# Router logits as four 32-column products in the attention's product bank, then one turn, in a relative-attention and mixture-of-experts kernel

## The chip, the cores and the metric

The kernel runs on one core of one Trainium2 chip. The time of a run is the device time in microseconds from the first to the last instruction and the little that lies around them. Three runs of the kernel before gave 1938.45, 1939.77 and 1939.66 us, median 1939.66 us. PE is the matrix engine (PEld its weight loads), DVE the vector engine, ACT the scalar engine, POOL the general engine, SP the engine that only issues transfers.

## The reference, cut to what matters

The input is 16 sequences (B) of 512 rows of 128 numbers, all float32. Each row goes through attention with relative positions, and then through a layer in which one of 16 experts is chosen for each row:

```python
x = x + _layernorm(attention(_layernorm(x)))          # 16 heads of 8, relative keys and values
h = _layernorm(x)                                     # rows of 128
logits = h @ w_router.T                               # [rows, 16]
_, top_idx = jax.lax.top_k(logits, 1)
scores = jax.nn.sigmoid(logits) * one_hot(top_idx)    # only the chosen expert's score is left
gate_up = (scores * h) @ gate_up_proj[expert]
expert_out = (up * silu(gate)) @ down_proj[expert]
shared = silu(h @ w_gate.T) * (h @ w_up.T) @ w_down.T
x = x + _layernorm(shared + expert_out)
```

The change is about the line of `logits`: 512 rows by 128 numbers by 16 experts for each sequence.

## The kernel before, in words

**Two stages.** The attention stage fills most of the span. It also chooses the experts ("the route") and scatters each row to a table in memory that is ordered by expert. The second stage reads that table in 73 blocks of 128 rows and runs the experts. The change lies in the first stage alone.

**The steps.** A sequence `b` is cut into 4 pieces `c` of 128 queries and each piece into 4 parts `n`, so it has 16 steps, `k` = 0 to 15, and the loop at L760 runs 256 steps and 24 more that empty the pipeline. The order of the instructions on every engine is that of the program (class `InOrder`, L39): no scheduler moves anything. In step `i` PE does, in this order:

- the scores of step `i` (`scores`, L375): four products `ps<-km,qb` of 32 rows by 512, and then 16 short products `ps<-relk,qr` for the relative keys;
- the first eight turns (transposes) of the weights of step `i - 1` (`turn`, L418), `pt<-ident,w`;
- the output products of step `i - 5` (`attend`, L471): 16 values' products `pa<-wT,v`, which show as 32 records of a 32-column tile (a float32 product takes two passes, a turn takes one), and 24 small products `pa<-wT,relv` for the relative values (`attend_near`, L503), 48 records;
- eight more turns;
- one extra that depends on `k` (L773 to L789, `spare`): the next sequence's projections, the turn of the reciprocal sums (`prt`), or the output projection (`py`, `output`, L538);
- what the route asks for (L833 to L847).

DVE meanwhile finds four maxima (`nmax`), copies two of the turned tiles out (`wT`), and takes in what `attend` made: `od`, `oz` and the sum `oT` (L494 to L499). ACT takes the exponentials and copies the other two turned tiles.

**The bank.** The scores have five PSUM buffers and the turned tiles two, but everything else shares a single one, the pool `ps_o` with `bufs=1` (L102, `bank`, L218). `attend` writes three thirds of it: `every3[:, 0]` for the values' products, `every3[:, 2]` for the relative values, and `every3[:, 1]` for `join_places`. Whoever takes the bank next waits until DVE has read it.

**The model for the new products.** In each step with `n == 1`, `attend` is given a finished piece `done`, and `join_places` (L459) runs four products of 128 rows by 32 columns, one to each 32-partition strip of `every3[:, 1]`, between the values' products and the relative values' products. DVE copies the result to `oj` between `oz` and `oT`. In the same step, after the second eight turns, `output` reads `oj` on PE.

**The route.** `route` (L595) is a generator for one sequence, which the loop advances at set steps. For sequences 0 to 13 (`r[0] < B - 2`, L837) the fifth call, at the end of step `k = 10` of the next sequence, is `turn_x2` (L639): four turns of the normalized rows, which ACT copies to `x2T`. The sixth, at the end of step `k = 11`, is `logits` (L648): four products with `x2T` as the loaded operand (128 columns each) and the 16 columns of `wr` streamed past it, into `pl`, which DVE copies to `lg`. Later calls find the largest logit, count the rows of each expert (`places`) and scatter the rows by indirect transfers that POOL issues (`rows<-pay,at_i`), of which two run in the steps 9 and 11 of the sequence after. The last two sequences follow another timetable. What follows `lg` is the same for all.

Of the kernel before, what the change touches and what calls it, by code (L numbers as in the profile page):

```python
# [9 lines left out]
F32 = mybir.dt.float32  # L10
# [7 lines left out]
P = 128  # L18
# [10 lines left out]
NC = P // 32  # L29
NE = 16  # L30
# [20 lines left out]
def relative_attention_then_moe(  # L51
# [6 lines left out]
    nc = tc.nc  # L58
    B = x.shape[0]
# [6 lines left out]
    ident = const.tile([P, P], F32, name="ident")  # L66
# [27 lines left out]
    with ExitStack() as actx:  # L94
        wp = actx.enter_context(tc.tile_pool(name="attn_w", bufs=1))
        dp = actx.enter_context(tc.tile_pool(name="attn_dram", bufs=1, space=DRAM))
        bp = actx.enter_context(tc.tile_pool(name="attn_batch", bufs=2))
# [5 lines left out]
        pe, act, dve, sp_q, pool = (InOrder(tc, e) for e in (nc.tensor, nc.scalar, nc.vector, nc.sync, nc.gpsimd))  # L103
# [68 lines left out]
        def later_loads():  # L172
            sp_q.dma_start(vext[0:127, :], rel_v[0:1, :].to_broadcast([127, HD]))
            sp_q.dma_start(vext[127 : 127 + NR, :], rel_v)
            sp_q.dma_start(vext[384:LR, :], rel_v[NR - 1 : NR, :].to_broadcast([LR - 384, HD]))
            va = vext[:, :]
            sp_q.dma_start(
                relv.rearrange("p t d -> p (t d)"),
                bass.AP(va.tensor, va.offset, [[HD, P], [1, 384 * HD]]),
            )  # L180
            sp_q.dma_start(wo, WoT)
            wo_v = WoT.rearrange("(g h d) o -> h g d o", g=HG, h=HH)
            for h in range(HH):
                for g in range(HG):
                    r = h * 32 + g * HD
                    sp_q.dma_start(wo_h[r : r + HD, :], wo_v[h, g])
            sp_q.dma_start(bo_r, bo.partition_broadcast(P))
            sp_q.dma_start(wr, w_routerT)


        mh = wp.tile([P, H], F32, name="mh")
# [22 lines left out]
        msum = wp.tile([P, HG, HD], F32, name="msum")  # L214

        batch, wts = {}, {}

        def bank(shape, name):  # L218
            return ps_o.tile(shape, F32, tag="o", name=name)
# [239 lines left out]
        def join_places(pj, b, c):  # L459

            oz = batch.pop((b, c, "oz"))
            for h in range(HH):
                pe.matmul(
                    pj[h * 32 : (h + 1) * 32, :], msum.rearrange("p g d -> p (g d)"),
                    oz[:, h].rearrange("p n t q -> p (n t q)"), start=True, stop=True,
                )
            oj = up.tile([P, P], F32, tag="oj", name=f"oj{b}_{c}")
            batch[b, c, "oj"] = oj
            return lambda: dve.tensor_copy(oj, pj)

        def attend(b, c, n, done=None):  # L471


            wT = wts[b, c][0]
            v = batch[b]["v"]
            Rh = batch[b, c, "R"][0]
            if n == 0:
                batch[b, c, "oT"] = up.tile([P, NKT * 4, TQ], F32, tag="oT", name=f"oT{b}_{c}")
            oT = batch[b, c, "oT"]
            every3 = bank([P, 3, P], f"pa{b}_{c}_{n}")  # L480
            pa = every3[:, 0]
            for kt in range(NKT):
                vn = 1 if kt <= n - 2 else 2 if kt >= n + 2 else 0
                for g in range(HG):
                    r = slice(g * 32, (g + 1) * 32)
                    pe.matmul(
                        pa[r, :], v[:, vn, kt, r], wT[:, n, g, (kt - n) % NKT, :],
                        start=(kt == 0), stop=(kt == NKT - 1),
                    )
            t = slice(n * 4, n * 4 + 4)  # L490
            summed = join_places(every3[:, 1], *done) if done is not None else lambda: None
            near_done = attend_near(every3[:, 2], b, c, n)

            def leave():  # L494
                od = up.tile([P, 4, HH, TQ], F32, tag="od", name=f"od{b}_{c}_{n}")
                dve.tensor_mul(od, pa.rearrange("p (t h q) -> p t h q", h=HH, q=TQ), Rh[:, t])
                near_done()
                summed()
                dve.tensor_reduce(oT[:, t], od.rearrange("p t h q -> p t q h"), AX.X, ALU.add)  # L499

            return leave
# [54 lines left out]

        wr = wp.tile([P, NE], F32, name="wr")
        order = wp.tile([P, NE], F32, name="order")  # L560
        nc.gpsimd.iota(order, [[-1, NE]], base=NE, channel_multiplier=0, allow_small_or_imprecise_dtypes=True)
        ids = wp.tile([P, NT], I32, name="ids")
# [32 lines left out]
        def route(b, c0=0, c1=NC):  # L595
# [5 lines left out]
            nc_, pieces, nm = c1 - c0, slice(c0, c1), f"{b}_{c0}"  # L601
# [34 lines left out]
            yield  # L636
            x2T = bp.tile([P, nc_ * P], F32, tag="x2T", name=f"x2T{nm}", bufs=1)

            def turn_x2():  # L639
                pt = bank([P, nc_ * P], f"ptf{nm}")  # L640
                for t in range(nc_):
                    pe.transpose(pt[:, t * P : (t + 1) * P], x2[:, t, :], ident)
                return lambda: act.copy(x2T, pt)

            yield turn_x2
            lg = sp.tile([P, nc_, NE], F32, tag="lg", name=f"lg{nm}")

            def logits():  # L648
                pl = bank([P, nc_, NE], f"pl{nm}")
                for t in range(nc_):  # L650
                    pe.matmul(pl[:, t, :], x2T[:, t * P : (t + 1) * P], wr, start=True, stop=True)
                return lambda: dve.tensor_copy(lg, pl)

            yield logits

            shape = [P, nc_, NE]
            mx = sp.tile([P, nc_], F32, tag="mx", name=f"mx{nm}")
# [98 lines left out]
        if B > 1:  # L756
            load_x(1)
        later_loads()
        routes = {}
        for i in range(total + 24):  # L760
            b, c, n = at(i)
# [4 lines left out]
            done = at(i - 9)[:2] if n == 1 and 0 <= i - 9 < total else None  # L766
# [3 lines left out]
            if 0 < b < B and k == 6:  # L770
                routes[b - 1, 0] = route(b - 1)

            if i == total + 1:  # L773
                routes[b - 1, 0] = route(b - 1, 0, NC - 1)
            if i == total + 5:
                routes[b - 1, 1] = route(b - 1, NC - 1, NC)
# [7 lines left out]
            if nxt is not None:  # L784
                if k == 0 and b + 2 < B:
                    load_x(b + 2)
                if k in (6, 7, 14, 15):
                    f = {6: x_turn, 7: queries, 14: keys, 15: values}[k]
# [17 lines left out]
            if old is not None:  # L806
                attend(*at(old), done=done)()
            elif done is not None:
                join_places(bank([P, P], f"pj{b}"), *done)()
# [44 lines left out]
    with ExitStack() as fctx:  # L854
        wp = fctx.enter_context(tc.tile_pool(name="ffn_w", bufs=1))
# [7 lines left out]
        pe, act, dve, pool = (InOrder(tc, e) for e in (nc.tensor, nc.scalar, nc.vector, nc.gpsimd))  # L863
# [182 lines left out]
```

## Time and profile before

| What | Value |
|---|---|
| Median of three runs | 1939.66 us |
| The profiled execution | 1937.03 us, span 1935.3 us |
| Granted PE clock, mean of the span | 0.989 |
| Busy PE, DVE, ACT, POOL | 1867.6, 1528.0, 1208.7, 992.1 us |
| PE busy from 100 to 1600 us | 1492.89 us |
| `pl<-wr,x2T` on PE | 128 records, 16.6 us |
| `pa<-oz,msum` on PE | 504 records, 25.3 us |
| `lg<-pl` on DVE | 17 copies, 3.8 us |

Busy time is the time in which at least one instruction of the engine runs, so products that overlap are counted once. A group's mean duration is longer than the distance from one record to the next, as the products are pipelined; the distance is what a record costs, and is read from the starts in the timeline. "Idle before" is the time in which the engine stood still ahead of a group, with the instruction that ended the wait. "Issue" stands for a wait that the profile ties to nothing.

The steps are very regular. Taken from the starts of `ps<-km,qb`, the step `k = 12` lasts 6.15 us in each of the 16 sequences, and the sixteen steps of a sequence add up to about 102.6 us.

### The profile page before, as it was taken

The page shows a single profiled execution, that of the slowest core. Times are in us where ns is not written, and L with a number is a line of the kernel's source. Part 1 is how long each engine was busy: PE and PEld are TensorE (multiplying, and loading weights), DVE is VectorE, ACT ScalarE, POOL GpSimd, SP SyncE. Part 2 cuts the span into 40 slices and gives each one's busy share as a digit, 9 for nine tenths or more (in the row PEclk, how much of TensorE's full clock was granted, in tenths as well). Part 3 has the DMA queues.
Part 4 walks back from the last instruction along what each step waited for, and adds up shares of the span by engine and source line. Part 5 has one row for each costly group of instructions (what it writes and reads, how often), then busy time and mean ns, then how long its engine had stood idle before and what let it go on. Part 6 is the DMA issues. An engine that isn't in the chain of part 4 may idle for free. (4 is left out here: it accounts for less than half of the span.)

```text
span 1935.3 us, 88211 instructions
## 1 busy us (share of the span) xinstructions
PE 1867.6 (96%) x38254; PEld 1391.1 (72%) x38254; DVE 1528.0 (79%) x3995; ACT 1208.7 (62%) x3077; POOL 992.1 (51%) x1388
## 2 busy tenths in 40 slices
PE   6999999999999999999999999999999999779997
PEld 3667767777776777676767677777767676579997
DVE  4777787878787878787888878787879787757776
ACT  3666666666666666666666666666666665257775
POOL 4345455545454554546454555454645544236666
PEclk9999999999999999999999999999999999879999
DMA  2312000000000000000000000000000000066663
GB/s 77 69 31 52 4 24 4 17 12 11 17 5 24 5 24 3 25 3 25 3 24 5 24 4 20 9 13 16 5 18 4 18 3 9 8 172 182 183 180 89
DMA packets 88327, 68.64 MB, mean 35 GB/s; under 512 B 26439, under 2 KB 74340, under 8 KB 87808
## 3 DMA queue, kind: packets, MB, share of 16 engines
q1 hardware_dynamic: 81248, 53.60, 10.4%
q0 software_dynamic: 4384, 8.57, 1.3%
q8 instruction: 301, 4.93, 1.1%
q10 hardware_dynamic: 2304, 0.80, 0.2%
q14 instruction: 90, 0.74, 0.1%
HBM read 44.79 MB, written 18.75 MB: 33 GB/s over the span
## 5 line engine op out<-in xcount | busy, mean ns | idle before, releaser
L47 ACT ACTIVATE w<-ps,nmax 128x512 f32<-128x512 f32 x1024 | 700.1, 694 | 561.9 <-DVE nmax L47 561.4
L47 DVE TENSOR_REDUCE nmax<-ps 128x1 f32<-128x512 f32 x1024 | 655.7, 682 | 229.2 <-PE ps L47 228.0
L47 PE MATMUL pt<-ident,w 128*128 128x128 f32 x4096 | 561.5, 280 | 4.6 <-DVE wT L47 4.0
L47 PEld LDWEIGHTS pt<-ident,w 128*128 128x128 f32 x4096 | 439.1, 141 | 125.5 <-issue 85.6
L47 DVE COPY wT<-pt 128x512 f32<-128x512 f32 x512 | 348.7, 681 | 0.7 <-PE pt L47 0.7
L47 ACT COPY wT<-pt 128x512 f32<-128x512 f32 x512 | 301.6, 589 | 25.1 <-PE pt L47 23.4
L47 PE MATMUL ps<-km,qb 32*128 32x512 f32 x2048 | 297.7, 645 | 3.5 <-POOL qb L47 3.5
L47 PEld LDWEIGHTS ps<-relk,qr 64*32 64x32 f32 x8192 | 124.3, 106 | 226.6 <-issue 184.1
L47 PE MATMUL pa<-wT,v 128*32 128x128 f32 x8192 | 276.7, 276 | 2.5 <-DVE oz L47 1.4
L47 PE MATMUL ps<-relk,qr 64*32 64x288 f32 (+4 forms) x8192 | 274.8, 377 | 0.0
L47 PEld LDWEIGHTS pa<-wT,v 128*32 128x32 f32 x8192 | 208.1, 109 | 45.3 <-issue 37.1
L47 ACT ACTIVATION_READ_ACCUMULATOR w<-ps,nmax 128x1 f32 x1024 | 211.9, 207 | 0.0
L47 PE MATMUL pa<-wT,relv 128*32 128x48 f32 (+1 forms) x12288 | 199.4, 211 | 6.6 <-issue 6.5
L47 POOL TENSOR_TENSOR Rh<-R,mh 128x512 f32<-128x512 f32 x64 | 66.7, 1042 | 263.8 <-ACT R L47 263.8
L47 PEld LDWEIGHTS pa<-wT,relv 128*32 128x32 f32 x12288 | 187.7, 110 | 10.8 <-issue 10.8
L47 POOL TENSOR_TENSOR qr<-qz,mq 128x1024 f32<-128x1024 f32 x64 | 137.4, 2147 | 0.0
L47 PEld LDWEIGHTS ps<-km,qb 32*128 32x128 f32 x2048 | 82.5, 184 | 58.6 <-issue 32.0
L47 POOL TENSOR_SCALAR km<-kT,kend 128x32 f32<-128x32 f32 (+2 forms) x223 | 116.4, 524 | 1.7 <-PE ps L47 0.9
L47 POOL COPY km<-kT 128x32 f32<-128x32 f32 (+3 forms) x207 | 53.6, 263 | 113.8 <-ACT kT L47 113.8
L47 POOL DMA_INDIRECT out_dram<-f,to x73 | 75.9, 1040 | 46.1 <-issue 32.3
L47 POOL COPY rb<-rt 128x512 f32<-128x512 f32 x64 | 39.4, 616 | 114.9 <-DVE rt L47 114.7
L47 DVE TENSOR_TENSOR od<-pa,Rh 128x128 f32<-128x128 f32 x256 | 73.2, 286 | 30.4 <-PE pa L47 26.9
(162 smaller groups left out, 2341.7 us busy)
## 6 DMA issues: line engine op xcount, KB each, us to landing
gu<-_L_ffn_gate_up_proj_dram SPq DMA_DIRECT2D x73, 256.0 KB
dn<-in_L_ffn_down_proj_dram SPq DMA_DIRECT2D x73, 128.0 KB
rows<-zero SPq DMA_DIRECT2D x19, 266.0 KB
xc<-rows SPq DMA_DIRECT2D x8, 532.0 KB
x_sb<-in_L_attn_x_dram SPq DMA_DIRECT2D x64, 64.0 KB
qd<-qp SPq DMA_DIRECT2D x16, 256.0 KB
qz<-qd SPq DMA_DIRECT2D x248, 16.0 KB
relv<-vext SPq DMA_DIRECT2D x1, 1536.0 KB
```

Of the source, the lines that this page charges most:

```text
L47: return lambda *a, **k: self.tc.keep_in_program_order(op(*a, **k))
```

## The change

For the sequences 0 to 13 the logits are made in another way:

- `wr` becomes 32 columns wide; the 16 new ones are zero (a memset on POOL at the start), and the load of the router's weights fills the first 16.
- When `turn_x2` runs, it puts `logits_tiles` on a list, `riders`. The next `attend` without a piece to join takes it: four products with `wr` (32 columns) as the loaded operand and the 128 columns of each quarter of `x2T` streamed past it, one to each strip of the free third of the bank, behind the values' products and ahead of the relative values' products of step 11. The result is the logits with experts as rows.
- DVE copies that third, 128 by 128, to a new tile `lgT`, between `oz` and `oT` of the same step.
- At the place of the old `logits`, one turn of `lgT` puts rows back as rows, and DVE copies the 16 real columns of each quarter to `lg`.

The order of the changed program has, for each of the 14 sequences, the four products and the turn on PE in place of the four old products, and one copy more on DVE. On POOL there is the one memset more, on ACT and SP nothing differs.

```diff
-            sp_q.dma_start(wr, w_routerT)
+            sp_q.dma_start(wr[:, 0:NE], w_routerT)
...
+        riders = []
...
             t = slice(n * 4, n * 4 + 4)
-            summed = join_places(every3[:, 1], *done) if done is not None else lambda: None
+            summed = lambda: None
+            if done is not None:
+                summed = join_places(every3[:, 1], *done)
+            elif riders:
+                summed = riders.pop()(every3[:, 1])
             near_done = attend_near(every3[:, 2], b, c, n)
...
-        wr = wp.tile([P, NE], F32, name="wr")
+        wr = wp.tile([P, 32], F32, name="wr")
+        nc.gpsimd.memset(wr, 0.0)
...
+            lgT = bp.tile([P, P], F32, tag="lgT", name=f"lgT{nm}", bufs=1) if b < B - 2 else None
+
+            def logits_tiles(pn):
+
+                for t in range(NC):
+                    pe.matmul(
+                        pn[t * 32 : (t + 1) * 32, :], wr, x2T[:, t * P : (t + 1) * P], start=True, stop=True
+                    )
+                return lambda: dve.tensor_copy(lgT, pn)
+
             def turn_x2():
+                if b < B - 2:
+                    riders.append(logits_tiles)
                 pt = bank([P, nc_ * P], f"ptf{nm}")
...
-                    pe.matmul(pl[:, t, :], x2T[:, t * P : (t + 1) * P], wr, start=True, stop=True)
+                    pe.matmul(pl[:, t, :], x2T[:, t * P : (t + 1) * P], wr[:, 0:NE], start=True, stop=True)
                 return lambda: dve.tensor_copy(lg, pl)
 
-            yield logits
+            def turn_logits():
+                pl = bank([P, NC, 32], f"pl{nm}")
+                pe.transpose(pl.rearrange("p c e -> p (c e)"), lgT, ident)
+                return lambda: dve.tensor_copy(lg, pl[:, :, 0:NE])
+
+            if b < B - 2:
+                yield turn_logits
+            else:
+                yield logits
```

## The prediction

> **What bounds the kernel now.** I read the windows by stage first, then PE's groups, then the timeline of the step that is changed. In the windows, from 100 to 1600 us (columns: window, length, then busy time of PE, PEld, DVE, ACT, POOL) PE is busy for 1492.89 of 1500 us, DVE for 1233.70:
>
> ```profile
> 100.00:1600.00 1500.00, 1492.89 (x33268) 1068.36 (x33270) 1233.70 (x3174) 963.72 (x2475) 780.99 (x1026) 1.00 0.06 14
> ```
>
> So in this stretch a PE microsecond more or less should be a microsecond of the span. Busy time alone doesn't prove that, so here is a second look: step 11 of sequence 6, PE in order of time (start, length, group, count).
>
> ```profile
> 704.96 1.14 PE L47 MATMUL ps<-km,qb 32*128 32x512 f32 x8
> ...
> 707.87 1.08 PE L47 MATMUL pa<-wT,v 128*32 128x128 f32 x32
> 708.77 0.38 PE L47 MATMUL pa<-wT,relv 128*32 128x64 f32 x16
> 709.33 0.62 PE L47 MATMUL pa<-wT,relv 128*32 128x48 f32 x32 [0.18 <-issue]
> 709.88 1.09 PE L47 MATMUL pt<-ident,w 128*128 128x128 f32 x8
> 710.81 0.96 PE L47 MATMUL pl<-wr,x2T 128*128 128x16 f32 x8
> 711.70 1.14 PE L47 MATMUL ps<-km,qb 32*128 32x512 f32 x8
> ```
>
> The step runs from 704.96 to 711.70, 6.74 us. In sequence 1 the same step runs from 192.21 to 198.54, 6.33 us, as it has no pause in the relv products (there 196.01 to 196.69; here 708.77 to 709.88, 0.43 longer). Yet step 12 behind it lasts 6.15 us in both (198.54 to 204.69; 711.70 to 717.85). PE time that is spared in step 11 is thus kept: nothing in step 12 waits for another engine to catch up. That is the reason why I count PE's starts and little else.
>
> **What the change removes.** Four products, eight records. From the start of pl at 710.81 to the next ps at 711.70 they hold PE for **0.89 us** (sequence 1: 197.62 to 198.54, 0.92).
>
> **What it adds on PE: the products.** The nearest row has the same shapes, loaded 128x32, streamed 128x128, four strips, at the same place between v and relv: `pa<-oz,msum`. In step 9 of sequence 6:
>
> ```profile
> 694.61 1.08 PE L47 MATMUL pa<-wT,v 128*32 128x128 f32 x32
> 695.50 0.40 PE L47 MATMUL pa<-oz,msum 128*32 128x128 f32 x8
> 695.72 0.28 PE L47 MATMUL pa<-wT,relv 128*32 128x64 f32 x5
> 696.20 0.77 PE L47 MATMUL pa<-wT,relv 128*32 128x64 f32 x43 [0.20 <-issue]
> 696.91 1.09 PE L47 MATMUL pt<-ident,w 128*128 128x128 f32 x8
> 697.92 0.46 PE L47 MATMUL py<-wo,oT 128*128 128x128 f32 x2
> ```
>
> 695.50 to 695.72: **0.22 us** for eight records, since the strips run beside each other. The ends: 0.22 by distance, 0.40 by busy time (25.3 us for 63 sets); I take the distance, as the next group starts there.
>
> **The pause.** Steps 9 and 11 hold an "issue" pause in their relv products, from sequence 2 on, and in both a `rows<-pay,at_i` of POOL starts just before: at 694.92 in step 9, at 708.17 in step 11, about 0.6 to 0.7 us ahead of the end of the v products. Sequence 1 has neither the transfer nor the pause. Relv takes 1.19 us with it in step 9 (695.72 to 696.91) against 0.68 without (step 13: 722.19 to 722.87), 0.51 more; in step 11 it is 0.43 more. After the change step 11 is laid out like step 9, products first, so I give it step 9's pause: **0.08 us** more. Ends: the pause is missed altogether (-0.43), or is as long as in the longest step 9 (7.31 us against the usual 7.13 to 7.14 by the starts of ps): +0.26.
>
> **The turn.** One more 128x128 pass behind eight like it. From 709.88 to 710.81 a pass takes 0.93 / 8 = 0.12; four prt passes ahead of ps take 0.53 (717.32 to 717.85), so the last one before ps costs 0.53 - 3 x 0.11 = **0.20 us**, and the single turn is such a last one.
>
> **The wait that it adds.** The turn reads lgT, so PE waits for DVE. What DVE does in step 11 now, and in step 9, where oj stands at lgT's place:
>
> ```profile
> 709.99 0.29 DVE L47 TENSOR_TENSOR od<-pa,Rh 128x128 f32<-128x128 f32 x1 [0.16 <-PE pa L47]
> 710.20 0.28 DVE L47 TENSOR_TENSOR oz<-pa,Rz 128x128 f32<-128x128 f32 x1
> 710.39 0.38 DVE L47 TENSOR_REDUCE oT<-od 128x32 f32<-128x128 f32 x1
> 710.69 0.68 DVE L47 COPY wT<-pt 128x512 f32<-128x512 f32 x1
> ```
>
> ```profile
> 697.49 0.28 DVE L47 COPY oj<-pa 128x128 f32<-128x128 f32 x1
> ```
>
> od moves by 0.22 + 0.08 to 710.29, oz to 710.50, lgT to 710.69 (at oT's distance), and ends 0.28 later at 710.97. In step 9 oj ends at 697.77 and py starts at 697.92, so DVE's end to PE's start takes 0.15: the turn can start at 711.12. PE has done its eight turns at 709.88 + 0.30 + 0.93 = 711.11. The wait is **0.01 to 0.02 us**. Its ends are 0 and 0.15, what it would be if the turns in between were 0.13 shorter; it is small only because eight turns cover the DVE chain. Queued behind the waiting turn is all of PE, ps of step 12 first.
>
> **What DVE pays.** lgT's copy takes 0.20 by distance. It delays oT and the wT copy, so with the 0.30 above wT ends at 711.87 and lg, rt follow by 712.2. rt feeds POOL's rb (0.61) and that prt, which PE reaches about 5.6 us into step 12: over 4 us of slack. The turned tile's buffer is wanted again by the first pt of step 12, some 2.1 us into it, and is free by 0.6. The next nmax starts 1.8 us into step 12. All hidden; if that cover were gone, 0.2 a sequence, 2.8 us in all.
>
> **Nothing else.** The memset on POOL (0.11) falls ahead of a 1.85 us idle time (before lx_rs at 7.57). The wr load has as many bytes as before. x2T is there 0.8 us into step 11, the products come 3.8 us in. Sequences 14 and 15 and the expert stage only start earlier.
>
> **The sum.** For sequences with the pause, 13 of the 14: -0.89 + 0.22 + 0.08 + 0.20 + 0.01 = -0.38. For the first, which has none: -0.92 + 0.22 + 0.20 + 0.02 = -0.48. Together 13 x 0.38 + 0.48 = **5.4 us**. The profiled execution has a span of 1935.3 and took 1937.03, so its like would take 1931.6. It ran 2.6 us below the median of the runs, and from the median, 1939.66, the forecast is **1934.3 us**.
>
> **A rule that speaks against it.** The eight products' loads span 0.24 us in step 9's PEld rows though each lasts 0.110, so loads and passes overlap. The Trainium skill, TensorE: Matmul & The Clock Gate, Part 3 (packing small matmuls), says that a weight load overlaps with running products only where the row group differs, and all four strips here use all 128 rows. By that rule this change is the last rival below; the trace disagrees with it, 0.22 us for eight.
>
> **The rivals.**
> - *The pause is as now, or is missed* (0.17). Then 13 x 0.46 + 0.48 = 6.5 us are spared, 1933.2; without any pause 13 x 0.89 + 0.48 = 12, 1927.6. For it: the pause hits one spot in time, and 0.22 us of other products now stand in front of relv. Against: step 9, laid out the same, is hit in every sequence from 2 on.
> - *The pause grows* (0.09). It falls where PE's instructions are shortest (relv, 14 ns apart), and there are 16 more ahead of them (loads counted). With the longest step 9's +0.26 in place of 0.08: 13 x 0.20 + 0.48 = 3.1 us spared, 1936.6.
> - *PE time isn't what counts, or the products don't ride in step 11* (0.04). Then the time stays at 1939.7. Against: step 12's equal length, and the order of the changed instructions, which has them there.
> - *The strips run one after another* (0.02), which ends slower. Each pass would take its load and itself, 0.110 + 0.273 = 0.38, eight 3.06 instead of 0.22, so 2.84 - 0.38 = 2.5 more a sequence, 14 x 2.5 = 34 us, 1974. It is slower from the point where the eight take over 0.60. Against: 63 sets of oz products at 0.22.
>
> **How the numbers follow.** The forecast has 0.68. About 0.2% (3.9 us) is what a measurement can tell from no change, so faster means below 1935.8. The forecast and the first rival are faster, 0.85; the second and third are the same, 0.13; the last is slower, 0.02. The range for 8 in 10 takes in the first rival's unchanged pause and part of its missed one, and the grown pause: 1931.2 to 1936.8.
>
> **What would show it.** In the changed profile: a group `pa<-x2T,wr` (or its like) of 112 records and some 5.6 us busy; `pl<-wr,x2T` left with 16 records; step 11 from ps to ps at 6.36 instead of 6.74, and 5.85 in sequence 1; step 12 still 6.15; PE idle before the new turn under 0.05 each; relv in step 11 at about 1.19. Wrong would be: a step 12 that grows by what step 11 lost, a turn that waits 0.2 or more for lgT, or a pause of another length.

## The result, and the profile after

| | before | after |
|---|---|---|
| median of 6 runs each, us | 1939.79 (1938.45 to 1942.64) | 1931.65 (1928.05 to 1932.57) |
| profiled execution, us (its span) | 1937.03 (1935.3) | 1931.33 (1929.6) |
| after over before | | 0.9952, 95% interval 0.9940 to 0.9965 |

The kernel after is 9.3 us faster by the ratio, with 6.8 and 11.6 as the ends of its interval (the medians lie 8.1 apart); 5.4 had been forecast. The sign and the place are right, the size is too small. The two profiled executions lie 5.7 us apart, which looks like the forecast and is an accident: sequence 0, from its first `ps` to that of sequence 1, took 99.39 us in the one and 101.78 in the other, and in three profiles of the unchanged kernel before it took 99.39, 99.85 and 103.38. In the profile after, PE's granted clock is 0.5 from 97.6 to 101.0 us, in sequence 0. So I compare steps, not spans. A step is the time from the first `ps<-km,qb` of one step to that of the next; the table has the median over sequences 2 to 13.

| step | before | after | difference, us |
|---|---|---|---|
| 11 | 6.744 | 6.186 | -0.558 |
| 12 | 6.153 | 6.156 | 0.003 |
| 9 | 7.134 | 7.133 | -0.001 |
| 4 | 6.130 | 6.106 | -0.024 |
| 0 | 6.146 | 6.131 | -0.015 |
| all 16 | 102.584 | 101.984 | -0.600 |

Sequence 1, where no scatter runs beside step 11, went from 6.33 to 5.90, 0.43 less. So 13 x 0.60 + 0.43 = 8.2 us is what the steps explain, within the interval.

The windows by stage first (window, length, then busy time of PE, PEld, DVE, ACT, POOL). PE is busy for 1495.02 of the 1500 us, so it is still what the time hangs on; DVE has 6.5 us more; the 14 new copies are among it, and so is work of later steps that moved into the window:

```profile
100.00:1600.00 1500.00, 1495.02 (x33459) 1064.92 (x33448) 1240.24 (x3199) 967.03 (x2485) 782.14 (x1030) 1.00 0.06 14
```

The groups by line and shape show that the change is all there: 14 sequences with eight records of products and one turn, and only the last two sequences' old products:

```profile
L47 PE MATMUL pa<-x2T,wr 128*32 128x128 f32 x112 | 5.6, 273 | 0.0
...
L47 PE MATMUL pl<-ident,lgT 128*128 128x128 f32 x14 | 4.2, 300 | 0.0
L47 PE MATMUL pl<-wr,x2T 128*128 128x16 f32 x16 | 3.1, 320 | 1.0 <-ACT x2T L47 1.0
```

Step 11 of sequence 6 in order of time (start, length, group). It runs from 704.06 to 710.25, 6.19 us:

```profile
704.06 1.14 PE L47 MATMUL ps<-km,qb 32*128 32x512 f32 x8
...
706.97 1.08 PE L47 MATMUL pa<-wT,v 128*32 128x128 f32 x32
707.86 0.40 PE L47 MATMUL pa<-x2T,wr 128*32 128x128 f32 x8
708.08 1.07 PE L47 MATMUL pa<-wT,relv 128*32 128x64 f32 x48
709.08 1.09 PE L47 MATMUL pt<-ident,w 128*128 128x128 f32 x8
710.02 0.30 PE L47 MATMUL pl<-ident,lgT 128*128 128x128 f32 x1
710.25 1.14 PE L47 MATMUL ps<-km,qb 32*128 32x512 f32 x8
```

Read from start to start: the products take 0.22 as forecast (707.86 to 708.08), the turn 0.23 (710.02 to 710.25). The relative values' products take 1.00 (708.08 to 709.08), where the forecast had 1.19 and the kernel before 1.11. The pause is inside this group; by the single records nothing starts from 708.15 to 708.43, 0.28 us (median of the 12 sequences 0.27), where the kernel before has 0.39. POOL's rows and DVE's of the same step:

```profile
707.24 1.12 POOL L47 DMA_INDIRECT rows<-pay,at_i  x1 [0.17 <-issue]
```

```profile
709.19 0.29 DVE L47 TENSOR_TENSOR od<-pa,Rh 128x128 f32<-128x128 f32 x1 [0.26 <-PE pa L47]
709.40 0.28 DVE L47 TENSOR_TENSOR oz<-pa,Rz 128x128 f32<-128x128 f32 x1
709.60 0.28 DVE L47 COPY lgT<-pa 128x128 f32<-128x128 f32 x1
709.79 0.37 DVE L47 TENSOR_REDUCE oT<-od 128x32 f32<-128x128 f32 x1
```

`lgT` ends at 709.88, the turn starts at 710.02: 0.14 behind it, the forecast had 0.15. Eight turns before it took 0.94 instead of 0.93, so the wait is 0.01.

### The profile page after: what moved, and what is told of

Its sections match the earlier page's. It is cut to its first block, busy times and chain, and to the rows that moved or that the text cites. A ratio compares the mean times of both kernels' runs of the same rounds, so it can differ in the third digit from the quotient of the medians.

```text
span 1929.6 us, 88255 instructions
## 1 busy us (share of the span) xinstructions
PE 1863.7 (97%) x38268; PEld 1383.0 (72%) x38268; DVE 1528.7 (79%) x4009; ACT 1207.7 (63%) x3077; POOL 989.8 (51%) x1389
```

## The experiments

My theory after these traces: while POOL runs a scatter (`rows<-pay,at_i`, 1.1 us on POOL), PE gets no new instructions and lives on those that it holds; when they run out it pauses, until 1.16 to 1.30 us after the scatter's start. In the kernel before, step 11, 36 matmul records start between the scatter and the pause (with their loads 72 instructions), in step 9 33; after, 35 and 33. The eight new products stand among them and last 27 ns each, by distance, where relative values' products last 14. The same number of held instructions so lasts 8 x 13 ns = 0.11 us longer, the pause starts 0.11 later, and its end, which the scatter sets, stays. The Trainium skill, Advanced Engine Details and Errata, Engine Queue Depths, gives TensorE a queue of 64 instructions; with the loads these rows have 66 to 72, a little more. That page doesn't say that a scatter stops its supply; the theory is mine.

Two others stand against this queue theory. The rival: the pause is 0.11 shorter because the turn has taken the place of the old products, and the place of the new ones has nothing to do with it. The layout, from the prediction: with products ahead of the relative values' products, step 11 has step 9's pause, 0.08 longer.

The runs came in six groups, each on one chip. The table has the medians of steps as above, and the time with that of the kernel before in the same group. Where a kernel leaves out work, its time is not comparable and only the steps count. In groups 1 and 4, and for before_again, the time is that of a single run.

| group, kernel | step 4 | 6 | 9 | 11 | us | before beside it |
|---|---|---|---|---|---|---|
| result: before | 6.13 | 6.26 | 7.13 | 6.74 | 1939.79 | |
| result: after | 6.11 | 6.26 | 7.13 | 6.19 | 1931.65 | 1939.79 |
| 1 products_only | 6.13 | 6.26 | 7.16 | 6.93 | 1945.45 | 1941.25 |
| 1 turn_only | 6.12 | 6.26 | 7.17 | 6.07 | | |
| 1 products_behind | 6.13 | 6.27 | 7.13 | 6.32 | 1932.17 | 1941.25 |
| 1 after_two_scatters | 6.10 | 6.26 | 6.67 | 5.90 | | |
| 2 after_again | 6.11 | 6.26 | 6.67 | 5.90 | 1919.59 | 1926.38 |
| 2 before_two_scatters | 6.08 | 6.26 | 6.67 | 6.37 | | |
| 2 after_moved | 6.11 | 6.26 | 6.67 | 5.90 | 1920.07 | 1926.38 |
| 2 moved_copy_first | 6.10 | 6.26 | 6.67 | 5.90 | 1919.40 | 1926.38 |
| 3 before_again | 6.10 | 6.26 | 6.67 | 6.37 | 1924.14 | 1926.66 |
| 3 after_third | 6.10 | 6.26 | 6.67 | 5.90 | 1919.92 | 1926.66 |
| 3 moved_again | 6.11 | 6.26 | 6.67 | 5.90 | 1919.75 | 1926.66 |
| 3 three_in_six | 6.09 | 6.46 | 6.67 | 5.90 | 1920.63 | 1926.66 |
| 4 before_fourth | 6.13 | 6.26 | 7.16 | 6.76 | 1941.37 | 1941.69 |
| 4 moved_third | 6.12 | 7.70 | 6.67 | 6.60 | 1955.11 | 1941.69 |
| 4 three_fourth | 6.10 | 8.43 | 6.67 | 5.90 | 1954.17 | 1941.69 |
| 5 after_fourth | 6.10 | 6.26 | 7.11 | 6.17 | 1933.77 | 1940.49 |
| 5 reordered | 6.11 | 6.26 | 6.67 | 7.10 | 1938.37 | 1940.49 |
| 6 spread | 6.38 | 6.26 | 6.67 | 5.90 | 1924.65 | 1942.05 |

**The change in parts (group 1).** products_only keeps the old `logits` beside the new products:

```diff
-            if b < B - 2:
-                yield turn_logits
-            else:
-                yield logits
+            yield logits
```

> The changed kernel with the four products and the copy to lgT kept, but the logits made by the old four products as before (the new ones are then used by nobody). Times are step 11 of sequences 2 to 14, from one ps<-km start to the next; it is 6.74 us before and 6.19 changed, and the relv products in it take 1.11 and 1.00 us with a pause of 0.43 and 0.32. Queue theory: while POOL makes the descriptors of a scatter, about 1.2 us from its start, PE gets no new instructions and lives on some 64 that it holds; the pause is what is left when these are used up. The new products then add 0.22 and take 0.11 off the pause, since 16 of the instructions that are held are slower ones: 6.74 + 0.22 - 0.11 = 6.85, relv 1.00. Layout theory, the one of the prediction (a pause of its own length, 0.51, wherever products stand ahead of relv): 6.74 + 0.22 + 0.08 = 7.04, relv 1.19. Rival (the pause is shorter because of what stands behind relv, the turn in place of the old products): 6.74 + 0.22 = 6.96, relv 1.11.

Its step 11 in sequence 6 on PE:

```profile
711.04 0.40 PE L47 MATMUL pa<-x2T,wr 128*32 128x128 f32 x8
711.25 1.07 PE L47 MATMUL pa<-wT,relv 128*32 128x64 f32 x48
712.26 1.09 PE L47 MATMUL pt<-ident,w 128*128 128x128 f32 x8
713.20 1.04 PE L47 MATMUL pl<-wr,x2T 128*128 128x16 f32 x8
714.16 0.71 PE L47 MATMUL ps<-km,qb 32*128 32x512 f32 x4
```

711.25 to 712.26 is 1.01: the products by themselves shorten the pause by as much as in the kernel after, as the queue theory says; the rival and the layout do not. The step is 0.08 longer than I had expected, and that is all in the old products, 0.97 (713.20 to 714.16) where the kernel before has 0.89.

turn_only leaves the products out and turns a tile of zeros:

```diff
+        lgT0 = wp.tile([P, P], F32, name="lgT0")
+        nc.gpsimd.memset(lgT0, 0.0)
...
-            lgT = bp.tile([P, P], F32, tag="lgT", name=f"lgT{nm}", bufs=1) if b < B - 2 else None
+            lgT = lgT0
...
-                if b < B - 2:
-                    riders.append(logits_tiles)
```

> The changed kernel without the four products and without the copy to lgT; a tile of zeros is turned in its place, so the logits of sequences 0 to 13 are all zero and all their rows go to the first expert. Only the first stage is to be read. Queue theory: nothing stands ahead of relv, so the pause is 0.43 again: step 11 is 6.74 - 0.89 + 0.23 = 6.08, relv 1.11. Rival (the turn behind relv shortens the pause): 5.97, relv 1.00.

It came out at 6.07, with a pause of 0.41, as long as before: without the products nothing shortens it, and the rival's 5.97 is out. products_behind puts them after the relative values' products:

```diff
-            elif riders:
-                summed = riders.pop()(every3[:, 1])
             near_done = attend_near(every3[:, 2], b, c, n)
+            if done is None and riders:
+                summed = riders.pop()(every3[:, 1])
```

> The changed kernel with the four new products behind the relative values' products of step 11, not ahead of them. Queue theory: the instructions that PE holds when the scatter starts are v and relv again, so the pause is 0.43 and step 11 is 6.19 + 0.11 = 6.30. Rival (the products shorten the pause wherever they stand): 6.19. DVE's copy comes some 0.05 later against od than now at most, so the turn's wait stays under 0.1 in both.

```profile
707.58 0.38 PE L47 MATMUL pa<-wT,relv 128*32 128x64 f32 x16
708.15 0.59 PE L47 MATMUL pa<-wT,relv 128*32 128x48 f32 x30 [0.19 <-issue]
...
708.58 0.41 PE L47 MATMUL pa<-x2T,wr 128*32 128x128 f32 x7
708.92 1.09 PE L47 MATMUL pt<-ident,w 128*128 128x128 f32 x8
```

6.32 against 6.30 expected. The same products in the same step, but behind the pause, save nothing of it: nothing starts for 0.41 us, as in turn_only. DVE's copy to `lgT` is in this kernel as in the kernel after, so the copy isn't what shortens the pause. 0.13 us of a step hang on the products' place alone. What the scatter has to do with it, its absence shows:

```diff
+                if b < B - 2 and t >= 2:
+                    continue
                 own_rows("rows", pool.indirect_dma_start(
```

> The changed kernel without the third and the fourth scatter of the sequences 0 to 13: half of their rows never reach the table, and the rest of the program is as it was. Queue theory: no scatter, no pause: step 9 falls from 7.13 to 6.67 and step 11 from 6.19 to 5.90, the values of sequence 1, in all sequences; 13 x (0.46 + 0.29) = 9.8 us off the first stage. Rival (the pause belongs to the place in PE's instructions, for example to their fetch, or to other transfers): step 9 stays at 7.13 and step 11 at 6.19 from sequence 2 on.

> The kernel before without the third and the fourth scatter of sequences 0 to 13 (half of their rows never reach the table). Queue theory: step 9 is 6.67 and step 11 6.33 in all sequences from 1 to 14. Against the changed kernel without the same scatters (step 11 5.90) the change is then worth 0.43 a sequence, and the 0.55 that it is worth with the scatters holds 0.11 of pause. Rival: step 11 stays at 6.74, as its pause is not the scatter's.

```profile
705.89 0.75 PE L47 MATMUL pa<-wT,relv 128*32 128x64 f32 x48
706.57 1.09 PE L47 MATMUL pt<-ident,w 128*128 128x128 f32 x8
```

These rows are after_two_scatters, step 11 of sequence 6: the relative values' products take 0.68 (705.89 to 706.57) and have no pause. Step 9 falls to 6.67 and step 11 to 5.90, on the chip on which the other three kernels of group 1 have their pause. So there is no pause without the scatter. before_two_scatters gives 6.67 and 6.37, but shows nothing of this: it ran in group 2, where, as the next runs show, there is no pause with the scatters either.

**A surprise (groups 2 and 3).** I then moved the third and fourth scatter, to win the pause's time:

```diff
-                    turns = i - (r[0] + 1) * 16 - 6 in (0, 1, 2, 3, 4, 5, 6, 7, 12, 13, 14, 15, 16, 17, 19, 20, 21)
+                    turns = {21: 2}.get(
+                        i - (r[0] + 1) * 16 - 6,
+                        i - (r[0] + 1) * 16 - 6 in (0, 1, 2, 3, 4, 5, 6, 7, 12, 13, 14, 15, 16, 17),
+                    )
```

> The changed kernel once more, beside the others on one chip. The steps of sequences 2 to 14 should be as before to 0.02 us (step 11 6.19, step 9 7.13). If the difference between the profiled spans (5.7 us) and between the medians (8.1 us) comes from sequence 0, whose length was 99.4 us in the profile before and 101.8 in the profile after while PE stood at half clock for 3.4 us in it, then sequence 0 varies by some 1 to 3 us from profile to profile in both kernels, and the times here differ by 7 to 10 us. Rival: a steady loss of 2.4 us in sequence 0 belongs to the change; then the steps 11 and 12 of sequence 0 are again 2.4 longer than before, and the times differ by 6.

> The changed kernel with the scatters of sequences 0 to 13 at other places in POOL's order: two in step 6, one in step 7, one behind step 11's last key products, none in step 9 and none ahead of step 11's relv. Queue theory: a scatter that starts where PE's instructions are long costs nothing, as 64 of them last longer than its 1.2 us. Step 9 falls to 6.67, step 11 to 5.90; the second scatter of step 6 starts at about 2.9 us, ahead of the v products, and may cost up to 0.15 there. So 0.6 to 0.75 for each of 13 sequences, 8 to 10 us faster than the changed kernel. Rival (a scatter costs PE its 0.3 to 0.5 us wherever it falls): steps 6 to 8 and 11 grow by what step 9 loses, and the time stays.

> As after_moved, with DVE's copy to lgT ahead of od instead of behind oz, in the 0.26 us in which DVE waits for relv. The turn then waits for the bank's other readers alone. If the turn's late start and its load behind it (0.04 to 0.06 us now) are the whole cost of the wait, step 11 falls by 0.02 to 0.05, less than 0.7 us in all; if the wait is no cost at all, nothing changes; if the copy in front delays od by its 0.20, step 11 grows by as much.

Nothing of the gain came. The kernel after, unchanged, has no pause on that chip, and the kernel before beside it takes 1926.38 instead of 1939.79. The two moved versions tell nothing there but one thing: `lgT`'s copy ahead of `od` brings nothing, step 11 is 5.90 either way. To know whether the kernel before is free of the pause too, it was profiled in group 3, on a further chip, with the kernel after beside it:

> The kernel before, unchanged, for its profile on another chip. In the second group of runs no step 9 or 11 had a pause in its relative values' products although the scatters of POOL stood at the same places (3.54 and 3.18 us into the step), and all of its times were 13 us lower. If the pause belongs to the chip and not to the kernel, this run shows one of two: step 9 at 7.13 and step 11 at 6.74 with a time near 1940, or step 9 at 6.67 and step 11 at 6.33 to 6.37 with a time near 1926. If the pause belonged to the kernel before, this run would show it on any chip.

> The kernel after, unchanged, on the same chip as the run of the kernel before beside it. With the pause: step 9 at 7.13, step 11 at 6.19, about 1931. Without it: 6.67 and 5.90, about 1920. Its gain over before is 13 x 0.56 + 0.43 = 7.7 us with the pause and 13 x 0.47 + 0.43 = 6.5 us without.

before_again, step 11 of sequence 6, PE and then POOL:

```profile
702.10 1.14 PE L47 MATMUL ps<-km,qb 32*128 32x512 f32 x8
...
705.91 0.75 PE L47 MATMUL pa<-wT,relv 128*32 128x64 f32 x48
706.58 1.09 PE L47 MATMUL pt<-ident,w 128*128 128x128 f32 x8
707.51 1.03 PE L47 MATMUL pl<-wr,x2T 128*128 128x16 f32 x8
708.48 0.71 PE L47 MATMUL ps<-km,qb 32*128 32x512 f32 x4
```

```profile
705.30 1.12 POOL L47 DMA_INDIRECT rows<-pay,at_i  x1 [0.17 <-issue]
```

The scatter starts 3.20 us into the step and lasts 1.12, as on the chips with the pause, and the relative values' products take 0.67 (705.91 to 706.58). So the scatter is needed for the pause but is not enough. Each group ran on one chip, so the chip may have a part in it, or something else that differs from group to group. Which, these profiles don't show: the scatter's length, its place, its packets and the order of the instructions are the same. In what follows, "a chip without the pause" is one of these two, and no more is known of it. On these two chips the change is worth 6.37 - 5.90 = 0.47 a step, and the ratios are 0.9964 (0.9951 to 0.9976) and 0.9966 (0.9953 to 0.9978), some 6.5 to 7 us.

moved_again and three_in_six ran in the same group; the second puts three scatters one behind the other into step 6, at 1.8, 3.2 and 4.5 us:

```diff
-                    turns = i - (r[0] + 1) * 16 - 6 in (0, 1, 2, 3, 4, 5, 6, 7, 12, 13, 14, 15, 16, 17, 19, 20, 21)
+                    turns = {16: 1, 17: 3, 22: 1}.get(
+                        i - (r[0] + 1) * 16 - 6,
+                        i - (r[0] + 1) * 16 - 6 in (0, 1, 2, 3, 4, 5, 6, 7, 12, 13, 14, 15),
+                    )
```

> The kernel after with the third and fourth scatter of each sequence moved: one starts at 3.23 us in step 6, one at 3.65 in step 11, none is left in step 9. Theory of the 64 held instructions, on a chip with the pause: 34 matmul records (with their loads some 64 instructions) after 3.65 PE is at 4.27, the supply comes back 1.18 us after the scatter's start, at 4.82, so the pause in step 11 is about 0.55 and the step 6.45 (6.19 in the kernel after); step 9 falls to 6.67; in step 6 the 34th record is at 4.14 and the supply is back at 4.25 to 4.41, so step 6 is 6.36 to 6.53. Spared against after: 0.46 - 0.26 - 0.1 to 0.27, that is 0.1 to -0.07 a sequence, so hardly anything. Rival, that the pause stands at a fixed place of the step or comes from the products and not from the scatter: step 11 stays at 6.19 and step 9 at 7.13. On a chip without the pause: step 6 6.26, step 9 6.67, step 11 5.90, the same time as after.

> The kernel after with three of the four scatters of each sequence one behind the other in step 6 (at about 1.8, 3.2 and 4.7 us) and the fourth at the start of step 8, none in steps 9 and 11. On a chip with the pause: step 9 6.67, step 11 5.90; in step 6 the first scatter falls into 512- and 288-column products and the third into 128-column turns, where 34 records last 1.9 us and over 3 us, longer than the 1.2 us, so no pause; the second makes one of 0.1 to 0.27. Against after 0.46 + 0.29 - 0.1 to 0.27 = 0.48 to 0.65 a sequence, 6 to 8.5 us less. Rival, that any scatter costs PE its half microsecond wherever it stands: no gain, step 6 at 7.2 or more. On a chip without the pause: the same time as after.

Three in a row cost step 6 0.20 even there (6.46), so a chip without the pause isn't free of the scatter's pull: PE loses 0.08 in the products and 0.09 behind the turns, and DVE's `od` starts 0.32 us after the products' end, where 0.08 is usual.

**Where the pause follows the scatter (groups 4 and 5).** The same two kernels on a chip with the pause:

> The kernel before, unchanged, to see whether this chip has the pause. With it: step 9 7.13, step 11 6.74. Without: 6.67 and 6.37.

> The kernel after with scatters at 1.8 and 3.23 us in step 6, 0.2 in step 8, 3.65 in step 11, none in step 9. If the chip has the pause, theory of the held instructions: step 11 6.45 (pause 0.55 from 4.27 on), step 9 6.67, step 6 6.36 to 6.53. Rival, a pause at a fixed place of the step: step 11 6.19, step 9 7.13. Without the pause: 6.26, 6.67 and 5.90 as on the two chips so far.

> The kernel after with scatters at 1.8, 3.23 and 4.50 us in step 6, 0.2 in step 8, none in steps 9 and 11. If the chip has the pause: step 9 6.67, step 11 5.90, and step 6 above the 6.46 that it has without the pause, by 0.1 to 0.3. Without the pause: 6.46, 6.67, 5.90.

moved_third, step 11 of sequence 6, PE and POOL:

```profile
716.85 0.40 PE L47 MATMUL pa<-x2T,wr 128*32 128x128 f32 x8
717.07 0.37 PE L47 MATMUL pa<-wT,relv 128*32 128x64 f32 x13
717.90 0.65 PE L47 MATMUL pa<-wT,relv 128*32 128x48 f32 x35 [0.47 <-issue]
718.48 1.09 PE L47 MATMUL pt<-ident,w 128*128 128x128 f32 x8
```

```profile
716.71 1.12 POOL L47 DMA_INDIRECT rows<-pay,at_i  x1 [0.16 <-issue]
```

The scatter starts 0.48 us later in the step than in the kernel after, and the pause moves with it and grows: nothing starts from 717.23 to 717.90, which is 1.20 us after the scatter's start, as in the other steps. So a pause at a fixed place of the step is out too. But step 11 is 6.60, not 6.45: only 25 records start within the stop, not 34. And in step 6, where I had expected 6.36 to 6.53, two scatters make 7.70:

```profile
681.92 1.09 PE L47 MATMUL pt<-ident,w 128*128 128x128 f32 x8
682.94 1.08 PE L47 MATMUL pa<-wT,v 128*32 128x128 f32 x21
684.34 0.53 PE L47 MATMUL pa<-wT,v 128*32 128x128 f32 x10 [0.32 <-issue]
...
685.47 1.09 PE L47 MATMUL pt<-ident,w 128*128 128x128 f32 x8
686.85 0.63 PE L47 MATMUL ptx<-ident,xn 128*128 128x128 f32 x4 [0.28 <-DVE oz L47]
```

```profile
681.52 1.12 POOL L47 DMA_INDIRECT rows<-pay,at_i  x1 [1.11 <-DVE shift L47]
682.94 0.96 POOL L47 DMA_INDIRECT rows<-pay,at_i  x1 [0.30 <-issue]
```

The second scatter starts 0.30 us after the first has ended, and only 16 records start before PE stands still for the first time (682.94 to the gap at 683.40). My theory had PE hold the same number each time. My next guess: what PE holds is a reserve that is full only after some us of long instructions, and is eaten up by a scatter just before, or by short ones. That is not all of step 6, though, for DVE stands still there too:

```profile
684.43 0.69 DVE L47 COPY wT<-pt 128x512 f32<-128x512 f32 x1 [1.47 <-PE pt L47]
```

This copy starts 4.71 us into the step, and in moved_again, the same kernel on a chip without the pause, 3.16 us into it; ACT's copy of the other turned tiles starts at 4.77 instead of 4.02 (medians). Both wait for PE's semaphore, the signal that the eight turns are done. By the trace, which models PE's ends, the last turn ends at 683.01, but the semaphore is raised at 684.40, and DVE starts 0.02 after that; DVE's own semaphores in this step are raised within 0.02 us of the end of the instruction. So PE's signals are held up too, and a reserve of instructions doesn't explain that. Beside a lone scatter, the one at 1.8 us in step 6, PE's signal for the first four turns comes 3.25 us into the step in the kernel after and 2.87 in after_third (medians); there it costs the step nothing.

With three scatters in a row (three_fourth) step 6 is 8.43, and the kernel is 12 us slower than the kernel before (one run of each).

If the guess is right, a lone scatter in front of long products costs nothing. reordered changes one line, so that the third scatter stands behind the newer sequence's normalised rows, in step 10, and pushes the fourth to 4.5 us in step 11:

```diff
-            for r in sorted(routes):
+            for r in sorted(routes, reverse=k == 9):
```

> The kernel after, unchanged. On a chip with the pause: step 9 7.13, step 11 6.19, 7.7 us plus the first sequence's difference below before. Without it: 6.67 and 5.90, 6.5 us below.

> The kernel after with one line of the scheduling loop changed, so that the third scatter of a sequence stands on POOL behind the newer sequence's normalised rows: it should start at 5.5 us in step 10, ahead of the 128-column turns and the next 512-column products, and push qb, qr and km, and with them the fourth scatter, to about 4.5 us in step 11. From there 24 matmul records last beyond 6.4 us and 34 beyond 7.2, later than the 1.2 us after which the supply is back (6.7 in step 10, 5.7 in step 11), and no second scatter follows. Theory: on a chip with the pause step 9 is 6.67, step 10 6.43 and step 11 5.90, so 13 x (0.46 + 0.29) = 9.8 us less than after. Rival: wherever a lone scatter stands it costs PE its pause, or qb and qr, 1.1 us later, hold up step 12: then step 10, 11 or 12 grows by 0.3 or more and the gain is under 4 us. On a chip without the pause: the same as after, within 1 us.

Steps 10 and 11 of sequence 6 in reordered, POOL's two scatters, then PE around the second, then DVE:

```profile
705.39 1.12 POOL L47 DMA_INDIRECT rows<-pay,at_i  x1 [0.17 <-issue]
...
710.66 1.08 POOL L47 DMA_INDIRECT rows<-pay,at_i  x1 [0.17 <-issue]
```

```profile
710.15 0.75 PE L47 MATMUL pa<-wT,relv 128*32 128x64 f32 x48
710.83 1.43 PE L47 MATMUL pt<-ident,w 128*128 128x128 f32 x8
712.99 0.30 PE L47 MATMUL pl<-ident,lgT 128*128 128x128 f32 x1 [0.73 <-DVE lgT L47]
```

```profile
712.15 0.29 DVE L47 TENSOR_TENSOR od<-pa,Rh 128x128 f32<-128x128 f32 x1 [1.16 <-PE pt L47]
...
712.56 0.28 DVE L47 COPY lgT<-pa 128x128 f32<-128x128 f32 x1
```

The first scatter, 5.69 us into step 10, costs nothing: step 10 is 6.42 as ever and step 9 6.67. The second starts at the end of the short products, and step 11 is 7.10, 1.2 above the 5.90: six records start, then PE's turns stand 0.21 and 0.30 apart in two places, where 0.11 is usual. That is 0.3 us of the 1.2. Most of the rest comes through DVE: its `od`, whose input is done at 710.89, starts at 712.15, 0.41 us after the scatter's end, and the new turn waits 0.73 for `lgT` behind it. DVE itself is not stopped: in the trace PE's semaphore for that input is raised at 712.13, 1.24 us late, as in moved_third. My expectation of 5.90 for step 11 was wrong. That this scatter would stand right behind the short products could have been seen beforehand and would have told against it; 1938.37 against 1933.77 is a loss.

**The version that the experiments point to (group 6).** The fourth scatter goes to step 4 of the next sequence, ahead of `rb`, where long products run; the third stays in step 10:

```diff
-            for r in sorted(routes):
+            for r in sorted(routes, reverse=k == 9):
...
-                    turns = i - (r[0] + 1) * 16 - 6 in (0, 1, 2, 3, 4, 5, 6, 7, 12, 13, 14, 15, 16, 17, 19, 20, 21)
+                    turns = i - (r[0] + 1) * 16 - 6 in (0, 1, 2, 3, 4, 5, 6, 7, 12, 13, 14, 15, 16, 17, 19, 29, 30)
```

> The kernel after with the third scatter in step 10 (as in the run before this one, where it started at 5.7 us and cost nothing) and the fourth in step 4 of the next sequence, behind km's copies and ahead of rb, so from about 1 us on: lone scatters, each in front of products or turns that are long, after some 4 us without short instructions. Theory of PE's reserve (it is full when long instructions ran before the scatter, and is drained by the short ones of the value phase): on a chip with the pause steps 4, 9, 10 and 11 are 6.10, 6.67, 6.42 and 5.90, 13 x (0.46 + 0.29) = 9.8 us below after and 17 to 18 us below before, a ratio of 0.991. Rival, a scatter always costs the same: step 4 is 0.5 to 1.2 longer and the gain over after is under 4 us. On a chip without the pause: the same as after, 6.5 us below before.

Step 11 of sequence 6 on PE, without a pause on a chip that has it (the kernel before takes 1942.05 beside it):

```profile
705.30 0.40 PE L47 MATMUL pa<-x2T,wr 128*32 128x128 f32 x8
705.52 0.75 PE L47 MATMUL pa<-wT,relv 128*32 128x64 f32 x48
706.20 1.09 PE L47 MATMUL pt<-ident,w 128*128 128x128 f32 x8
707.17 0.30 PE L47 MATMUL pl<-ident,lgT 128*128 128x128 f32 x1
707.40 0.71 PE L47 MATMUL ps<-km,qb 32*128 32x512 f32 x4
```

It takes 1924.65 us (1922.90 to 1925.84), 0.9908 of the kernel before beside it (0.9891 to 0.9924). The kernel after did not run on this chip; on two others with the pause it took 1931.65 and 1933.77. Steps 9, 10 and 11 are 6.67, 6.42 and 5.90 as expected. Step 4 is 6.38 instead of 6.10; the scatter leaves no gap in its products, but the turn of `rb` waits 0.20 us for DVE's `oz`:

```profile
662.38 0.63 PE L47 MATMUL prt<-ident,rb 128*128 128x128 f32 x4 [0.20 <-DVE oz L47]
```

DVE's first `nmax` starts 2.20 us into this step, 0.20 later than in the kernel after and just behind the scatter's end, and `oz` 0.27 later (medians). Here too it is PE's signal that is late: PE raises its semaphore for the scores at 2.17 and 2.22 us, and at 1.69 and 1.74 in the kernel after. The 0.27 us by which step 4 grows is the rival's sign at a quarter to a half of its size, and the theory of PE's reserve does not have it. That this chip has the pause rests on the kernel before beside it, which took 1942 and not 1926; its profile was not taken here.

## Why the prediction was right or wrong, point by point

The terms of step 11, medians of sequences 2 to 13, from start to start on PE:

| term | forecast | with the pause (before, after) | without (before_again, after_third) |
|---|---|---|---|
| old products away | -0.89 | -0.894 | -0.962 |
| new products | +0.22 | +0.218 | +0.219 |
| relative values' products with the pause | +0.08 | -0.127 (1.118 to 0.991) | -0.001 (0.678 to 0.677) |
| turns, with the wait for `lgT` | +0.01 | +0.010 | +0.039 |
| the new turn | +0.20 | +0.230 | +0.230 |
| sum | -0.38 | -0.563 | -0.475 |

- **Right: what bounds the kernel.** PE's starts carry the end; step 12 stayed at 6.15 while step 11 lost 0.56, so every spared bit was kept.
- **Right: what goes, the products, the wait, the cover.** 0.22 for the four products was the distance in the `oz` rows of step 9, and it holds to 2 ns. The last rival, strips one behind another, would have made these 3.06; it is out. By the rule of the Trainium skill that the prediction weighed (TensorE: Matmul & The Clock Gate, Part 3) the loads would not have overlapped; the trace after, with 0.22 for eight records, disagrees as that of before did. DVE's copy was covered as said.
- **Slightly off: the new turn,** 0.23 for 0.20. The forecast priced it as the last of four turns; in turn_only, without the copy to `lgT` ahead of it, it took 0.203, so the wait costs it 0.03. In sequence 1 the change is worth 0.43, where 0.48 had been forecast: the new turn's 0.03 and a wait of 0.04 in place of 0.02 make the difference.
- **Wrong: the pause.** The step that failed is "After the change step 11 is laid out like step 9, products first, so I give it step 9's pause: 0.08 us more." It came out 0.13 shorter, so 0.21 a sequence, 13 x 0.21 = 2.7 us, which is nearly all of the distance from the forecast's 5.4 to the steps' 8.2. The layout does not set the pause. Laid out alike, the kernel after has no start for 0.42 us in step 9 and for 0.27 in step 11, and most of the difference lies in the end: in step 9 the stop lasts 1.27 to 1.30 us from the scatter's start, in step 11 1.16 to 1.18. The end of the stop hangs on the scatter, its beginning, by the theory of the experiments, on how long the instructions that PE holds last, and longer ones ahead of the short ones last longer. The stretch in which no product starts went from 0.39 us to 0.27. I had written the argument down as the first rival's ("the pause hits one spot in time, and 0.22 us of other products now stand in front of relv") and drew no size from it: it had the pause unchanged or missed, 6.5 or 12 us spared, and the truth lies between. The second rival, the grown pause, had the sign of the effect the wrong way round: 16 more instructions ahead of the short ones do not bring the pause forward; it begins 0.11 us later in the step. The median of 1931.65 lies inside the range, near the end that had been drawn for a pause missed in part; no size for that had been worked out, so it is luck as much as judgement.
- **Outside the model: the chip.** That the pause could be absent with the scatter in place I had not thought of. There, on the chips of groups 2 and 3, the change is worth 13 x 0.475 + 0.43 = 6.6 us, and 6.8 and 6.7 were measured by the medians of groups 2 and 3; the terms without the pause give 0.46 in the forecast's own prices. On the chip of group 5, which has the pause, after_fourth is 6.7 us below the kernel before (ratio 0.9965, 0.9952 to 0.9979), where 7.7 had been expected. So whole times can't tell a gain of 0.56 a step from one of 0.47; the steps can.
- **Not a term at all: sequence 0.** A profiled execution's own time varies by 4 us in sequence 0 alone. The forecast's difference was put on the median of the runs, and there it can be judged; the two profiled spans hide 2.4 us of it.

Settled: the pause needs the scatter, moves with it, and is shortened by the new products put in front of the short ones. Argued, and not more: that PE lives on a reserve of instructions. It gave the right pauses in group 1 and missed in groups 4 to 6. Open: why two of the chips don't have the pause, and through what the scatter stops PE's starts and holds up its signals. A wait for the transfers that bring instructions does not explain the pause: the profile shows them (kind `instruction`), and in 11 of the 24 steps 9 and 11 of sequences 2 to 13 of the kernel before none runs between the scatter's start and the pause's end, and the pause is there all the same. The packets of the scatter move only after the pause (in the kernel before, 4.9 us into step 11, where the pause ends at 4.37), so its data isn't what stands in the way; the Trainium skill, Perfetto Trace Analysis, DMA Instruction — SWDGE (GPSIMD), says that such an instruction's window is the writing of its descriptors and not the moving of the data, and these rows agree.

## What to carry to other kernels

A pause that the profile puts down to "issue" has a beginning and an end with different causes; find both before giving a changed step the pause of a step that only looks alike. Where a scatter of POOL runs beside a PE that is always busy, put it alone in front of long products and not behind short ones or behind another scatter. Over the same kernel without a pause (101.2 us a sequence), the same four scatters, by their place, cost a sequence 0.28 us (spread), 0.75 (after), 1.2 (reordered) or 2.2 (three_fourth). What is left in spread is a late signal of PE, for which DVE waits. Compare steps rather than spans, and take the kernel before on the same chip: it took 1926 us on two chips and 1940 to 1942 on others.

## What the runs showed of the hardware

- In the profiles of the result and of groups 1, 4 and 5, a scatter of 128 rows by 532 bytes (1.07 to 1.12 us on POOL in steps 9 and 11) is followed by a pause of PE that ends 1.16 to 1.30 us after the scatter's start (medians). PE starts 33 to 36 matmuls within that stop, and 25 when the scatter stands behind 0.7 us of products that are 27 ns apart.
- On these chips PE's semaphores come late beside a scatter, 1.25 to 1.49 us after its start (medians; step 4 of spread, step 6 of after and moved_third, step 11 of reordered), though the products that they stand for had ended before by the trace, in which PE's ends are modelled. DVE's come within 0.02 us of the end of the instruction in step 6 of moved_third.
- On the chips of groups 2 and 3 the same kernels show no pause in steps 9 and 11, with the same scatters beside them, and ran 12 to 16 us faster.
- In the kernel before the pause adds 0.44 us to the relative values' products but 0.37 to the step, as the old four products take 0.89 us there and 0.96 without the pause. Why is open: in products_only, behind a shorter pause, they take 0.97.
